# Gated cross-attention block: the order of the last two head pairs' scores, values and outputs

## The chip, the cores and the metric

The kernel runs on one NeuronCore of one Trainium2 chip. The metric is the device time of one execution in microseconds (us). Names of engines: TensorE (PE in the profile), VectorE (DVE), ScalarE (ACT), GpSimd (POOL), SyncE (SP), which here only issues DMAs.

## The reference

`x` (32 batches of 64 tokens, width 512) attends to a context of the same shape, and a feed-forward layer with LoRA adapters follows, both added back through a gate:

```python
x = x + tanh(g_xattn) * xattn(layernorm(x), ctx_4096, mask, bias)   # 32 heads of 128
x = x + tanh(g_ffn) * ffn(layernorm(x))
# xattn: q = h @ Wq, k = c @ Wk, v = c @ Wv
#        p = softmax(q @ k.T / sqrt(128) + bias, masked);  return (p @ v) @ Wo
# ffn:   y = x @ weight.T + bias, plus (x @ A.T) @ B.T of the batch's adapter
```

All of it is float32. The kernel reaches that precision by splitting each operand into a high part and a low remainder and adding three products (high by high, high by low, low by high).

## The kernel before, in words

The 2048 tokens are done in two halves (`p` = 0 and 1) of 1024 tokens, which are 8 tiles of 128. A half has a stage A and an attention stage; after the second half the feed-forward layer runs in four chunks of 512 tokens.

**Stage A** computes the keys and the values of all 32 heads for this half and stores them in DRAM. Heads go in pairs (`n` = 0 to 15). The key product of one pair (`unit`, L354) is a Strassen-like scheme with seven products p1 to p7 instead of eight; each product needs one split block of the context (tiles `c1p` for the second half) and one split block of the weight (tiles `wk`). Their results appear as psum tiles px, py, pv, pz. The context blocks of the second half are made by `next_blocks` (L455) while the first half's attention is still ending: a split is a cast on ACT (L89) and a subtraction (L90) on GpSimd, or on VectorE where the code says so; plain subtractions of raw blocks are L468. It waits twice on `gate`: block p5 needs the first entry, blocks p2 and p4 the second, since they take over tiles that the attention's last outputs still read. The weight blocks come from `prep` (L305) and `key_blocks` (L566), sums L288, casts L295 and low parts L299, all of their sums and low parts on GpSimd.

**Attention** (`attention`, L745) handles head pairs in order. For a pair `n`:

- `q_unit(n)` makes the queries (psum px, py, pv, pz, tile `qT`).
- `score` (L1051) makes the scores `ps` on TensorE. VectorE adds the bias tile `sm` (L814) and takes the row maximum (L816), GpSimd subtracts it (L817), ACT takes the exponential (L826). The bias is loaded by `load_bias` (L756, 2 x 256 KB) into one of two `sm` buffers, which the pair two before must have left, and GpSimd adds the mask to it (`bias_mask`, L765).
- `normed` (L830) sums the rows on VectorE (L836 to L838) and scales them on GpSimd (L839).
- `turned` (L853) transposes the probabilities in blocks of 32 on VectorE (L850, tile `tp`), loads the bias of pair `n + 2`, and puts the blocks in place with 16 ACT copies of 32 x 256 (L847, tile `pt`; `pz` for pair 14). Its argument `pace` says how many copies go at each step. For the pairs 14 and 15 together `last_turned` (L898) does both, with the second head of pair 15 placed by VectorE directly (also L847).
- `pv(n, cs)` (L944) multiplies by the values into `po` (L949), in four groups of eight 128-wide matmuls, `c` being the half of the tokens. ACT evicts the high part (L953) and VectorE the low part (L954), into `ch` and `cl`, or, for pairs 13 and 15, both into `cx`.
- `oproj` and, for the last four pairs two by two, `oproj2` (L997) multiply by the output weights into `pa`, 6 matmuls per pair and tile, and VectorE adds them to the accumulator `acc` (L993, L1008). `oproj2(n, ts, lead)` first issues pair `n`'s matmuls for `lead` tiles, then those of pair `n + 1`. The weights are split by `prep_o` (L965, tile `wo`, ACT L89 and GpSimd L90); when a pair's weights are split, it fetches the next pair's on SP.

**What sets the order.** [...] TensorE's order is written out by hand in `run` (L1022). The work of the other engines hangs on generators in the list `streams`; `beat()` (L64), called after each group of matmuls, advances each of them by one step. `paced(g, k)` takes a step only at every k-th beat. `drain(g)` issues all that is left of a generator at once. So the position of a stream's start decides where its instructions stand in the queues of ACT, VectorE, GpSimd and SP.

In the kernel before, the end of a half's attention is, in this order: outputs of pair 11, queries 14, values 12, queries 15, then `last_unit()` (it starts the blocks and first keys of the next half, or in the second half the splitting of the feed-forward weights, `ffn_weights`, L1158), scores of 14 and 15, values 13, outputs of 12 and 13 for six tiles, values of 14 and 15 for the first half of the tokens, outputs of 12 and 13 for the other two tiles, values of 14 and 15 for the second half, outputs of 14 and 15. In the second half `beside` (L1295) puts two things between the tiles of those last outputs: VectorE's normalization (`ffn_norm`, L132) and moments (L105, L106) and, by `ffn_tile` (L1185), TensorE's transposes of the first chunk (`tpf`, evicted to `fa`). The adapter product `ffn_lora` (psum `pt`, L1197) follows and needs all four of these.

Of the kernel before, what the change touches and what calls it, by code (L numbers as in the profile page):

```python
# [23 lines left out]
NPH = 2  # L24
# [19 lines left out]
def flamingo_block(ctx: ExitStack, tc: tile.TileContext, x, xT, ctxT, bias, mask, gx, gf,  # L44
# [410 lines left out]
    def next_blocks(f, tags, nm, out, gate):  # L455
# [22 lines left out]
        while not gate:  # L478
            yield
        yield from block("p5", b11)  # L480
        while len(gate) < 2:
            yield
        yield from block("p2", b21, nc.vector)
        yield from sub(b21, b21, b22, nc.vector)
        yield from block("p4", b21, nc.vector)

# [258 lines left out]
    def attention(p, res, rest, qt, freed):  # L745
# [152 lines left out]
        def last_turned():  # L898
# [14 lines left out]
            for k in range(16):  # L913
                if k in (1, 3, 6, 8):
                    next(norm)
                if k in (4, 5):
                    turn_next(n, k - 4)
                if k in (5, 7):
                    zero(k // 7)
                if k == 9:  # L920
                    turn_next(n + 1, 0)
                if k > 5:
                    for of, m, i, q in todo[:3]:
                        copy(nc.scalar.copy, m, i, of, *q)
                    del todo[:3]
                if k > 10:
                    for m, i, q in direct[:2]:
                        copy(nc.vector.transpose, m, i, sm[m % 2][:, i], *q)
                    del direct[:2]
                yield  # L930
# [6 lines left out]
        def ctx_of(n):  # L937
# [4 lines left out]
            return ch, cl  # L942

        def pv(n, cs=(0, 1)):  # L944
            drain(b["s", n])
            for i, c in [(i, c) for i in range(2) for c in cs] if n == 0 else [(i, c) for c in cs for i in range(2)]:
                ps = psum(f"po{p}_{n}_{i}_{c}")
# [8 lines left out]
            if n + 1 < NPR - 1:  # L956
                load_v(n + 1)
                if ("n", n + 1) in b:
                    drain(b["n", n + 1])
                    b["s", n + 1] = turned(n + 1)  # L960
                    next(b["s", n + 1])
                    next(b["s", n + 1])
                    streams.append(b["s", n + 1])

        def prep_o(n):  # L965
# [5 lines left out]
            b["o", n] = t  # L971
            for i in range(2):
                sl = slice(i * 512, (i + 1) * 512)
                split(raw[:, sl], t[:, 0, sl], t[:, 1, sl], nc.gpsimd)
                yield
# [46 lines left out]
        def run(xq, prefetch, before_last, last_unit, values_read, beside=None):  # L1022
# [8 lines left out]
            def q_unit(n):  # L1031
# [13 lines left out]
                end()  # L1045
                if n == NPR - 1:
                    last_unit()
                elif n % 2 and n > 3:
                    start_q(n + 1)
# [38 lines left out]
            for a in range(4, NPR, 2):  # L1088
# [8 lines left out]
                if a < NPR - 2:  # L1097
                    pv(a - 1)
                score(a, a + 1)
                if a == NPR - 8:  # L1100
                    streams.append(paced(prefetch(), 4))

            n = NPR - 4
            load_v(n + 3)
            pv(n + 1)
            start_o(n + 2)
            oproj2(n, range(6), 3)
            start_o(n + 3)
            for c in range(2):
                if c:  # L1110
                    oproj2(n, range(6, NT), 1)
                pv(n + 2, (c,))
# [129 lines left out]
    for p in range(NPH):  # L1242
# [10 lines left out]
        if p < NPH - 1:  # L1253
# [10 lines left out]
            def last_unit():  # L1264
                nonlocal blocks
                blocks = paced(next_blocks(f, qt, f"c{p + 1}", first[0], gate), 2)
                keys = prep("k", g, nc.gpsimd, 34, then=lambda: fetch("k", g + 2, "r0"))
                streams.extend((blocks, keys))
# [8 lines left out]
        else:  # L1277
# [17 lines left out]
            def beside(t):  # L1295
                if t < 4:
                    ffn_norm(0, t)
                    moments(t)
                else:
                    ffn_tile(0, t - 4)  # L1300
                if t == 4:
                    rstd_of(NPH * NCH - 2)

            def rest_of(t):
                if t < 2:
                    moments(4 + 2 * t)
# [57 lines left out]
```

## Time and profile before

| | |
|---|---|
| median of 3 runs | 1549.71 us (1549.27 to 1550.78) |
| the profiled execution | 1549.48 us, span of its instructions 1547.70 us |
| TensorE busy | 1529.2 us (99%), mean granted clock 0.996 |
| VectorE, ScalarE, GpSimd busy | 948.0 (61%), 719.2 (46%), 1041.8 (67%) |
| first half: values 13 begin / next half's first key product | 677.68 / 742.58 |
| second half: values 13 begin / first transpose of chunk 1 | 1412.78 / 1480.73 |

Times are counted from the first instruction of the span. The busy share of TensorE comes from pipelined matmuls, so it does not say that TensorE works at its peak; where it truly waits is in the timeline, in brackets ahead of the instruction that waited. The granted clock is 1.00 at full speed and 0.50 when the array's clock is halved.

### The profile page before, as it was taken

How to read it: one execution, taken by the hardware profiler on the slowest of the kernel's cores; microseconds unless marked ns; L12 is line 12 of the kernel's file. 1: busy time of each engine (PE TensorE's matmuls, PEld its weight loads, DVE VectorE, ACT ScalarE, POOL GpSimd, SP SyncE). 2: the span in 40 equal slices, each digit the busy share in tenths (PEclk: the TensorE clock that was granted, in tenths of full speed). 3: DMA queues.
4: the chain of work that ended last, by engine and by line, in shares of the span. 5: the costliest groups of instructions: out<-in, count | busy, mean ns of one | idle time of the engine just before them, and what ended most of it. 6: DMA issues, size and time to landing. Idle time of an engine off the chain costs nothing.

```text
span 1547.7 us, 25053 instructions
## 1 busy us (share of the span) xinstructions
PE 1529.2 (99%) x8988; PEld 1285.1 (83%) x8988; DVE 948.0 (61%) x1583; ACT 719.2 (46%) x1586; POOL 1041.8 (67%) x1152
## 2 busy tenths in 40 slices
PE   9999999999999999999999999999999999999899
PEld 7888888888888888877788888888888888888777
DVE  5665554376576657655486558437657665766654
ACT  6444233355664565464334423335566456547321
POOL 3898478968666666666689847896866666666210
PEclk9999999999999999999999999999999999999999
DMA  5754544484243444441475454438425344444111
GB/s 212 264 191 150 199 169 171 142 315 163 89 173 136 145 169 163 152 137 55 146 276 191 150 200 170 171 142 310 162 90 181 132 149 165 167 147 131 42 41 69
DMA packets 111071, 248.51 MB, mean 161 GB/s; under 512 B 10241, under 2 KB 44033, under 8 KB 106850
## 3 DMA queue, kind: packets, MB, share of 16 engines
q1 hardware_dynamic: 110658, 246.38, 45.7%
q8 instruction: 71, 1.16, 0.3%
q10 hardware_dynamic: 288, 0.52, 0.1%
q14 instruction: 54, 0.44, 0.1%
HBM read 173.45 MB, written 73.42 MB: 160 GB/s over the span
## 4 chain that ended last, share of the span: by engine, by line
PE 91%; DVE 3%; POOL 2%; issue 1%; DMA 1%; ACT 1%; SPq 0%; DVEq 0%; POOLq 0%; ACTq 0%
PE pa L98 21%; PE po L949 7%; PE pzv L98 6%; PE pvv L98 6%; PE pxv L98 6%; PE pzk L98 5%; PE pvk L98 5%; PE pxq L98 5%; PE pxk L98 5%; PE pzq L98 5%; PE pvq L98 5%; PE ps L812 3%; PE pyv L98 3%; PE pyq L98 3%; PE pyk L98 3%; PE pf L98 2%
## 5 line engine op out<-in xcount | busy, mean ns | idle before, releaser
L98 PE MATMUL pa<-wo,ch 128*128 128x512 f32 x896 | 280.3, 394 | 0.0
L847 ACT COPY pt<-tp 32x256 f32<-32x256 f32 x456 | 183.9, 403 | 64.0 <-DVE tp L850 53.0
L98 PEld LDWEIGHTS pa<-wo,ch 128*128 128x128 f32 x896 | 167.5, 189 | 34.8
L98 PE MATMUL pa<-wo,cl 128*128 128x512 f32 x448 | 175.5, 392 | 0.0
L993 DVE TENSOR_TENSOR acc<-pa,acc 128x512 f32<-128x512 f32 x192 | 129.3, 681 | 53.5 <-PE pa L98 53.5
L765 POOL TENSOR_TENSOR sm<-sm,madd 128x512 f32<-128x512 f32 x60 | 76.7, 1294 | 103.9 <-DMA sm<-bias 103.9
L949 PE MATMUL po<-pt,v 128*128 128x128 f32 x960 | 115.4, 278 | 8.5 <-ACT pt L847 4.4
L949 PEld LDWEIGHTS po<-pt,v 128*128 128x128 f32 x960 | 113.5, 194 | 11.8 <-ACT pt L847 5.7
L839 POOL TENSOR_TENSOR sm<-sm,r 128x512 f32<-128x512 f32 x64 | 66.9, 1045 | 77.5 <-DVE r L838 70.0
L954 DVE TENSOR_TENSOR cl<-po,ch 128x512 fp32r<-128x512 f32 x112 | 76.4, 691 | 47.4 <-ACT ch L953 47.0
L356 DVE TENSOR_TENSOR vt<-pvv,vt 128x512 f32<-128x512 f32 x64 | 44.1, 689 | 93.3 <-PE pvv L98 93.2
L98 PEld LDWEIGHTS pa<-wo,cl 128*128 128x128 f32 x448 | 84.5, 189 | 18.5 <-DVE cl L954 0.6
L90 POOL TENSOR_TENSOR wo<-rawo,wo 128x512 fp32r<-128x512 f32 x64 | 81.4, 1295 | 21.6 <-ACT wo L89 21.6
L817 POOL TENSOR_TENSOR sm<-sm,mx 128x512 f32<-128x512 f32 x64 | 67.0, 1050 | 40.8 <-DVE mx L816 40.8
L953 ACT CAST ch<-po 128x512 fp32r<-128x512 f32 x112 | 65.6, 590 | 59.7 <-PE po L949 58.0
L356 DVE TENSOR_TENSOR qT<-pvq,qT 128x512 f32<-128x512 f32 x64 | 44.1, 690 | 73.2 <-PE pvq L98 73.1
L356 DVE TENSOR_TENSOR kT<-pvk,kT 128x512 f32<-128x512 f32 x60 | 41.3, 688 | 71.6 <-PE pvk L98 71.4
L378 ACT COPY vt<-pxv 128x512 f32<-128x512 f32 x32 | 18.9, 589 | 131.0 <-PE pxv L98 131.0
L826 ACT ACTIVATE sm<-sm 128x512 f32<-128x512 f32 x60 | 38.0, 633 | 83.9 <-POOL sm L817 80.7
L356 DVE TENSOR_TENSOR qT<-pzq,qT 128x512 f32<-128x512 f32 x64 | 44.2, 691 | 37.8 <-PE pzq L98 37.6
L812 PEld LDWEIGHTS ps<-kB,qT 128*64 128x64 f32 x2048 | 61.3, 138 | 4.2 <-issue 2.1
L812 PE MATMUL ps<-kB,qT 128*64 128x64 f32 x2048 | 64.1, 223 | 0.3 <-DVE qT L356 0.3
(997 smaller groups left out, 3879.5 us busy)
## 6 DMA issues: line engine op xcount, KB each, us to landing
kd<-kT SPq DMA_DIRECT2D x64, 512.0 KB, 3.6
vd<-vt SPq DMA_DIRECT2D x128, 256.0 KB, 2.3
kB<-kd SPq DMA_DIRECT2D x32, 1024.0 KB, 9.7
v<-vd SPq DMA_DIRECT2D x32, 1024.0 KB, 7.7
rawq<-wq SPq DMA_DIRECT2D x32, 512.0 KB, 3.4
sm<-bias SPq DMA_DIRECT2D x64, 256.0 KB, 6.3
rawo<-wo SPq DMA_DIRECT2D x32, 512.0 KB, 3.6
rawk<-wk SPq DMA_DIRECT2D x31, 512.0 KB, 5.4
```

Source lines behind the costliest of these rows:

```text
L90: eng.tensor_tensor(lo, raw, hi.bitcast(F32), ALU.subtract)
L98: nc.tensor.matmul(ps, a, b, start=start and i == 0, stop=stop and i == 3 * n - 1, skip_group_check=True)
L356: nc.vector.tensor_tensor(o, ps, i, ALU.add)
L765: nc.gpsimd.tensor_tensor(t, t, masks[p][0], ALU.add)
L812: nc.tensor.matmul(ps[h * S:(h + 1) * S, t, :], qT[:, i, tok], kT[:, i, tok], start=True, stop=True)
L817: nc.gpsimd.tensor_tensor(s, s, mx.unsqueeze(2).to_broadcast([P, NT, S]), ALU.subtract)
L839: nc.gpsimd.tensor_tensor(t, t, r.unsqueeze(2).to_broadcast([P, NT, S]), ALU.mult)
L847: f(pts[n == NPR - 2][dst, i, :, src], of[src, :, ki * 32:(ki + 1) * 32])
L949: nc.tensor.matmul(ps[:, t * P:(t + 1) * P], b["v", n][:, c * 4 + t, i * P:(i + 1) * P], pts[n == NPR - 2][:, i, c * 4 + t, :], start=True ...
L953: nc.scalar.copy(h[:, i, sl], ps)
L954: nc.vector.tensor_tensor(lo[:, i, sl], ps, h[:, i, sl].bitcast(F32), ALU.subtract)
L993: nc.vector.tensor_tensor(acc[t], ps, acc[t], ALU.add)
```

## The change

Six edits, all at the two ends of attention:

1. In `pv` of pair 12, pair 13 is turned (its VectorE transposes and the load of pair 15's bias) before the values of pair 12 instead of behind them; the copies keep their place behind the values.
2. Ahead of the scores of 14 and 15, the rest of pair 13's copies and the two casts of its output weights are issued, and then all streams are set aside; they come back after the values of 13. `last_unit()` moves there too, from the end of queries 15.
3. All eight tiles of outputs 12 and 13 come before the values of 14 and 15, the first four tiles as one group.
4. `last_turned` normalizes at steps 0, 2, 6 and 8 rather than 1, 3, 6 and 8.
5. In `next_blocks`, the subtraction for block p4 goes to GpSimd before the second gate, and the split of p4 goes from VectorE to GpSimd. The wait of the first keys' stream goes from 34 to 18 beats.
6. In the second half, the transposes of the first feed-forward chunk come at the tiles 2 to 5 of the last outputs rather than 4 to 7, and the moments of the tiles 0 to 3 after tile 3; the scales of chunk 2 (15 small GpSimd steps) move into the first chunk.

```diff
@@ -478,11 +478,11 @@
         while not gate:
             yield
         yield from block("p5", b11)
+        yield from sub(b22, b21, b22)
         while len(gate) < 2:
             yield
         yield from block("p2", b21, nc.vector)
-        yield from sub(b21, b21, b22, nc.vector)
-        yield from block("p4", b21, nc.vector)
+        yield from block("p4", b22)
 
     f = [big(f"f{j}", [P, KT, 512], F32, f"c0_{j}") for j in range(2)]
     fetch("k", 0, "r0", 4)
@@ -911,7 +911,7 @@
                 nc.vector.memset(pts[1][h * S:(h + 1) * S, :, :, (1 - h) * S:(2 - h) * S], 0.0)
 
             for k in range(16):
-                if k in (1, 3, 6, 8):
+                if k in (0, 2, 6, 8):
                     next(norm)
                 if k in (4, 5):
                     turn_next(n, k - 4)
@@ -941,8 +941,17 @@
                 return more_ctx
             return ch, cl
 
+        def turn_pair(n, **pace):
+            drain(b["n", n])
+            b["s", n] = turned(n, **pace)
+            next(b["s", n])
+            next(b["s", n])
+
         def pv(n, cs=(0, 1)):
             drain(b["s", n])
+            if n == NPR - 4:
+                turn_pair(n + 1, pace=(0, 1, 2, 2, 3, 2, 2, 2, 2))
+                next(b["s", n + 1])
             for i, c in [(i, c) for i in range(2) for c in cs] if n == 0 else [(i, c) for c in cs for i in range(2)]:
                 ps = psum(f"po{p}_{n}_{i}_{c}")
                 for t in range(4):
@@ -956,10 +965,8 @@
             if n + 1 < NPR - 1:
                 load_v(n + 1)
                 if ("n", n + 1) in b:
-                    drain(b["n", n + 1])
-                    b["s", n + 1] = turned(n + 1)
-                    next(b["s", n + 1])
-                    next(b["s", n + 1])
+                    if n != NPR - 4:
+                        turn_pair(n + 1)
                     streams.append(b["s", n + 1])
 
         def prep_o(n):
@@ -969,9 +976,16 @@
             else:
                 t = kqp.tile([P, 2, 1024], F32R, tag="kq", name=f"wo{p}_{n}")
             b["o", n] = t
-            for i in range(2):
-                sl = slice(i * 512, (i + 1) * 512)
-                split(raw[:, sl], t[:, 0, sl], t[:, 1, sl], nc.gpsimd)
+            halves = [slice(i * 512, (i + 1) * 512) for i in range(2)]
+            if n == NPR - 3:
+                for sl in halves:
+                    nc.scalar.copy(t[:, 0, sl], raw[:, sl])
+                yield
+            for sl in halves:
+                if n == NPR - 3:
+                    nc.gpsimd.tensor_tensor(t[:, 1, sl], raw[:, sl], t[:, 0, sl].bitcast(F32), ALU.subtract)
+                else:
+                    split(raw[:, sl], t[:, 0, sl], t[:, 1, sl], nc.gpsimd)
                 yield
             if n + 1 < NPR:
                 fetch("o", p * NPR + n + 1, "r1")
@@ -1043,9 +1057,7 @@
                 if n == 1:
                     start_o(0)
                 end()
-                if n == NPR - 1:
-                    last_unit()
-                elif n % 2 and n > 3:
+                if n % 2 and 3 < n < NPR - 1:
                     start_q(n + 1)
 
             def score(*ns):
@@ -1096,19 +1108,28 @@
                 start_o(a - 1)
                 if a < NPR - 2:
                     pv(a - 1)
+                else:
+                    drain(b["s", a - 1])
+                    next(ob[a - 1])
+                    held = list(streams)
+                    streams.clear()
                 score(a, a + 1)
                 if a == NPR - 8:
                     streams.append(paced(prefetch(), 4))
 
             n = NPR - 4
             load_v(n + 3)
+            beat()
+            streams.append(ob[n + 1])
+            drain(ob[n + 1])
             pv(n + 1)
+            streams.extend(g for g in held if g is not ob[n + 1])
+            last_unit()
+            oproj2(n, range(4), 4)
             start_o(n + 2)
-            oproj2(n, range(6), 3)
+            oproj2(n, range(4, NT), 1)
             start_o(n + 3)
             for c in range(2):
-                if c:
-                    oproj2(n, range(6, NT), 1)
                 pv(n + 2, (c,))
                 pv(n + 3, (c,))
             values_read(acc)
@@ -1264,7 +1285,7 @@
             def last_unit():
                 nonlocal blocks
                 blocks = paced(next_blocks(f, qt, f"c{p + 1}", first[0], gate), 2)
-                keys = prep("k", g, nc.gpsimd, 34, then=lambda: fetch("k", g + 2, "r0"))
+                keys = prep("k", g, nc.gpsimd, 18, then=lambda: fetch("k", g + 2, "r0"))
                 streams.extend((blocks, keys))
 
             def values_read(acc):
@@ -1295,13 +1316,14 @@
             def beside(t):
                 if t < 4:
                     ffn_norm(0, t)
-                    moments(t)
                 else:
-                    ffn_tile(0, t - 4)
-                if t == 4:
+                    moments(t - 4)
+                if 1 < t < 6:
+                    ffn_tile(0, t - 2)
+
+            def rest_of(t):
+                if t == 0:
                     rstd_of(NPH * NCH - 2)
-
-            def rest_of(t):
                 if t < 2:
                     moments(4 + 2 * t)
                     moments(5 + 2 * t)
```

## The prediction

> **What bounds the kernel now.** I read the page first, then TensorE's own waits, the busy time by stretch, and the timelines of TensorE and GpSimd around the end of each attention half.
>
> ```profile
> PE 1529.2 (99%) x8988; PEld 1285.1 (83%) x8988; DVE 948.0 (61%) x1583; ACT 719.2 (46%) x1586; POOL 1041.8 (67%) x1152
> ...
> 588.03:660.60 72.57, 72.57 (x463) 61.74 (x463) 49.44 (x89) 41.43 (x94) 48.05 (x54) 1.00 0.44 153
> 677.68:742.58 64.90, 58.84 (x293) 49.25 (x289) 34.14 (x59) 28.00 (x60) 42.50 (x41) 0.95 0.28 93
> 1412.78:1480.73 67.95, 62.85 (x317) 51.93 (x313) 40.77 (x75) 26.82 (x55) 26.69 (x37) 0.95 0.19 62
> ```
>
> TensorE sets the time. In a regular stretch (588 to 661) it is busy without a gap at full clock, so only removed waits can gain. The two ends of attention, from pair 13's values on, hold idle time and a mean clock of 0.95. TensorE's timeline (start, duration, line, operation, in brackets the idle time before it):
>
> ```profile
> 686.88 1.22 PE L98 MATMUL pa<-wo,cx 128*128 128x512 f32 x3 [1.26 <-ACT cx L953]
> 689.10 5.12 PE L98 MATMUL pa<-wo,cx 128*128 128x512 f32 x15 [1.00 <-ACT cx L953]
> ...
> 706.31 1.16 PE L949 MATMUL po<-pt,v 128*128 128x128 f32 x8 [2.14 <-ACT pt L847]
> 709.13 1.98 PE L949 MATMUL po<-pt,v 128*128 128x128 f32 x8 [1.66 <-DVE pt L847]
> ...
> 1438.23 1.16 PE L949 MATMUL po<-pt,v 128*128 128x128 f32 x8 [2.25 <-ACT pt L847]
> 1441.25 2.08 PE L949 MATMUL po<-pt,v 128*128 128x128 f32 x8 [1.85 <-DVE pt L847]
> ```
>
> TensorE waits for pair 13's evicted context and then for the turned probabilities of pair 15. After each wait matmuls run at half speed (15 in about 5 us; normally 12 take 2.72). GpSimd shows why the softmax is late:
>
> ```profile
> 676.44 2.52 POOL L765 TENSOR_TENSOR sm<-sm,madd 128x512 f32<-128x512 f32 x2 [10.08 <-DMA sm<-bias]
> 678.90 1.05 POOL L817 TENSOR_TENSOR sm<-sm,mx 128x512 f32<-128x512 f32 x1
> 679.90 1.29 POOL L90 TENSOR_TENSOR c1p<-c,c1p 128x512 fp32r<-128x512 f32 x1
> 681.13 1.31 POOL L90 TENSOR_TENSOR wo<-rawo,wo 128x512 fp32r<-128x512 f32 x1
> 682.38 1.06 POOL L817 TENSOR_TENSOR sm<-sm,mx 128x512 f32<-128x512 f32 x1
> ...
> 1375.66 1.05 POOL L817 TENSOR_TENSOR sm<-sm,mx 128x512 f32<-128x512 f32 x1 [0.27 <-DVE mx L816]
> ```
>
> Pair 15's bias lands so late that its mask additions stand in front of the first max subtraction (L817), and splits (L90) stand between the others. In an ordinary pair (last line) they follow VectorE at 1.32 us each.
>
> **The Trainium skill.** "TensorE: Matmul & The Clock Gate", Part 1: the array's clock is halved after an idle window of about 3.4 us and comes back after a busy one, and the window runs freely. Here the half-clock stretches are 3.4 us (at 688.8 and 709.3) and 6.8 us (at 1439.7); the windows ahead of the first two were about a third and under a third busy, so a window need not be wholly idle. The same page, Architectural detail: ScalarE, VectorE and GpSimd take their work strictly in order, which agrees with L817 behind L90 above. "SBUF — State Buffer", two separate sides: VectorE with two SBUF inputs and GpSimd lock each other out; here 256-wide GpSimd steps take 0.74 us, and 1.17 to 1.23 beside VectorE's subtractions at 749 to 753.
>
> **The change, part by part.** Prices: output matmul 2.72/12 = 0.227 us; a pair's values 3.57 for both halves, 1.78 for one; GpSimd 1.29 (L90, L765, L468), 1.05 (L817, L839); ACT 0.48 to 0.53 per queued 512-wide cast, 0.415 per turned copy; VectorE 0.6 to 0.7 per 512-wide step.
>
> *1. Pair 13 turned ahead of pair 12's values.* The two VectorE transposes (1.30) move from 665.65 to about 661.4, behind the last addition of q14. The four evictions of pair 12 slip by at most 0.4 us; their outputs are not read before 681. SP: the two bias loads go out at about 662.8 rather than 668.08, now ahead of wo13 (512 KB), v13 and k16, which can't start before 666.4 anyway. At 6.3 to 8.3 us they land by 671, so the two mask additions are over by 673 and free GpSimd before the first maximum at 676.47. The copies still start after pair 12's values are read, and end at 675.2 as now, because eight of them stand behind the px copy that TensorE releases at 671.2.
>
> *2. No other stream among the scores.* GpSimd's four L817 then follow VectorE's maxima: 676.5, 677.8, 679.2, 680.5, ending at 681.55 (now 687.9). wo13's casts (2 x 0.6) run ahead of the exponentials, its two subtractions behind the first L839: 681.6 + 1.05 + 2.58 = 685.2. Pair 13's four casts queue behind the last exponential (682.1) and end at 684.2, their low halves at about 686.4.
>
> *3. Order on TensorE.* From 677.68: values 13 (3.57) to 681.3; pair 12's terms of tiles 0 to 3, 24 x 0.227 = 5.44, to 686.7. Then pair 13's terms: the first half's low parts are there at 684.1, wo13 at 685.2. No wait, with 1.5 us to spare. All eight tiles end at 703.0. Meanwhile the last two pairs turn: VectorE does the row sums (1.1 each), four turns or clears and the additions in order, the last direct transposes end at about 699; ACT makes 24 copies (9.96) and a few casts from 687.1, ending at about 699. TensorE asks for pair 14 at 703.0 (ready 694.8) and for pair 15 at 704.8 (ready 699). Both waits go, by about 6 us. The earlier last_turned steps (0 and 2 for 1 and 3) are in these times.
>
> *4. Output weights.* On SP wo14's load goes out behind wo13's subtractions (685.2; now 684.7), v14's behind it, landing near 693.3 at its 7.7 us, used at 703. wo14 is split behind the 24 copies, ready at 701.9; wo15's load follows it and lands 3.6 us later at 705.6, its low half is ready at 708.8 behind two more block subtractions. It is asked for at 710.2 + 2.72 = 712.9. ACT waits for that load between two casts of pair 14, which have 4 us to spare.
>
> *Sum.* From values 13: 3.57 + 96 x 0.227 + 4 x 1.78 + 96 x 0.227 = 54.2. The first half now takes 742.58 - 677.68 = 64.9: gain **10.7**. In the second half, 1412.78 to 1480.73 = 67.95 now; after, 54.2 + four transposes inside the tiles at 0.49 (3.21 less 2.72 in the trace) + the adapter's 8 x 0.227 = 58.0: gain 9.95. Its bias load and L817s move as in the first half, and its weight splits come after the copies.
>
> *5. Second half's tail.* The tiles of chunk 0 are turned two steps earlier, so the adapter's waits at 1478 (0.68, 0.22) go (already in the 9.95). New: the moments of tile 3 (0.8) stand between the last addition and the normalization that the next transpose needs: last matmul + 0.2 + 0.6 + 0.8 + 0.54 = 2.2 against 1.8 of adapter matmuls: 0.4 lost, leaving 9.55. GpSimd's 15 small steps for the scales (4.2 us) move later; their first reader is some 7 us behind.
>
> *6. Blocks of the next half.* The block stream starts nine beats later, and the key stream's own wait falls from 34 to 18. GpSimd has about 41 us of work from 681.6 to the first key product at 731.9, some 9 us of slack; k16 is ready near 720, and k17's load (SP, behind wo15's split at 708.8) has 20 us. Block p4's subtraction (2 x 1.29) goes there unhurried. But p4's own split moves from VectorE to GpSimd, in a place where TensorE already waits: now p4's product ends at 753.92 instead of 752.1. After: cast at 750.7, subtraction to 752.05, then a key sum (0.74) releases a key cast that stands in ACT ahead of p4's second cast (753.7), subtraction to 755.0, product at 755.5. Loss **1.6**. GpSimd is 2.6 us later for the key blocks behind, which lead by 4.4. Within these 4.1 us TensorE is busy 0.7, so about half the phases of a 3.4 us window halve the clock next, at 1.7: book 0.9. Bounds: -1.8 (nothing left to wait for) and +4.
>
> Total: 10.7 + 9.55 - 1.6 - 0.9 = 17.7. The profiled execution took 1549.48 us (span 1547.70 and 1.78 around it), 0.23 under the median. 1549.5 - 17.7 = **1531.8**.
>
> **Rivals.**
> - *The turning is still late* (15%). If only the bias delay went, the chain from the end of the scores to the last direct transpose would stay near 31.3 and 28.4 us (709.1 - 677.75; 1441.2 - 1412.8), against 27.1 that TensorE needs to pair 15: 4.2 + 1.3 of wait and one or two slow windows: 7 to 9 us back, 1540. For it: VectorE has new additions in the way. Against it: the L817s alone gain 6.3.
> - *The wait moves to wo15* (12%). Its load now leads its use by 11 us, before by 25. If GpSimd runs 6 us late, TensorE waits 2 to 3 us per half, perhaps with a slow window: 1537.
> - *Slower: GpSimd bounds the next key stage* (6%). A key unit costs it 11 x 0.74 = 8.1 of 9.52 us. The p4 splits put it behind; if it then met VectorE's lock often enough that a step's mean passed (9.52 + 1.3)/11 = 0.98 us for 15 units, the gain would be gone. At 1.18 us (13.0 per unit) in half of the units: 7 x 3.5 = 24.5, 1556. Against it: those VectorE subtractions leave the stage here.
> - *The order changes and nothing else* (1%), 1549.5: excluded if the waits are gone at all.
>
> The forecast itself has 66%, its own range 1529 to 1535. The floor, with every wait and slow window removed, is 1549.5 - 10.7 - 9.95 - 1.8 = 1527. The range 1528 to 1539 leaves out the slower case and half of the late turning. Faster by over 0.2% (about 3 us, what a measurement of this kernel can tell from no change): 0.93; within it 0.01; slower 0.06.
>
> **What would show it.** Right: L817 in steps of 1.3 us behind the maxima, the bias landing before 672, no wait before po of pair 15, clock 1.00 in both ends, 54 us from values 13 to the next key product, p4's product waiting for GpSimd at the start of the key stage. Wrong: bracketed waits at po or cx, half-clock windows there, GpSimd-released waits at pxk or pyk, or a wait for rawo.

## The result, and the profile after

| us | before | after |
|---|---|---|
| median (range), 5 runs each on one chip | 1549.27 (1547.70 to 1550.78) | **1532.18** (1530.62 to 1533.45) |
| profiled execution, its span | 1549.48, 1547.70 | 1530.62, 1528.82 |
| first half: values 13 to the next half's first key product | 64.90 | 54.39 |
| from there to the second half's values 13 | 670.21 | 671.99 |
| second half: values 13 to the first transpose of chunk 1 | 67.95 | 58.61 |
| rest of the span behind it | 66.97 | 66.63 |

The ratio of after to before is 0.989, with a 95% interval of 0.9876 to 0.9904: 17.1 us by the medians, where 17.7 were predicted. The two profiled spans differ by 18.88: gains of 10.51 and 9.34 in the two attention ends, 0.34 behind them and 0.47 ahead of them (where nothing was changed), less a loss of 1.78 in the key stage.

TensorE and GpSimd in the first line of the page (busy time, share of the span, instructions):

```profile
PE 1519.3 (99%) x8988; PEld 1280.5 (84%) x8988; DVE 941.6 (62%) x1579; ACT 718.4 (47%) x1586; POOL 1046.7 (68%) x1156
```

Busy time by stretch in the kernel after (start and end, length, then PE, PEld, DVE, ACT and POOL busy, granted clock, DMA share, GB/s):

```profile
677.21:731.59 54.38, 54.38 (x291) 46.86 (x289) 33.92 (x59) 28.20 (x61) 43.13 (x40) 1.00 0.33 111
731.59:745.00 13.41, 10.79 (x45) 7.98 (x44) 4.51 (x7) 6.39 (x15) 8.38 (x10) 1.00 0.05 20
1403.58:1462.18 58.60, 58.29 (x316) 49.77 (x313) 40.25 (x76) 26.48 (x55) 21.99 (x20) 1.00 0.22 72
```

The first and third lines are the two ends of attention. TensorE is now busy without a gap in the first and, but for 0.31 us, in the second, both at full clock. The gaps that are left have moved to the middle line, the start of the next key stage: 10.79 busy of 13.41. TensorE's timeline of the kernel after, where the waits were before and where the new ones are (brackets hold the idle time ahead of the instruction and what ended it):

```profile
686.35 5.60 PE L98 MATMUL pa<-wo,cx 128*128 128x512 f32 x24
...
702.67 1.95 PE L958 MATMUL po<-pz,v 128*128 128x128 f32 x16
704.46 1.95 PE L958 MATMUL po<-pt,v 128*128 128x128 f32 x16
...
741.11 0.73 PE L98 MATMUL pvk<-c1p,wk16p 128*128 128x512 f32 x2 [0.85 <-POOL c1p L90]
742.75 0.50 PE L98 MATMUL pvk<-c1p,wk16p 128*128 128x512 f32 x1 [0.92 <-ACT c1p L89]
744.11 0.74 PE L98 MATMUL pvk<-c1p,wk16p 128*128 128x512 f32 x2 [0.85 <-POOL c1p L90]
...
1434.40 1.95 PE L958 MATMUL po<-pt,v 128*128 128x128 f32 x16
...
1462.18 0.63 PE L137 MATMUL tpf<-ident,xn 128*128 128x128 f32 x4 [0.31 <-DVE xn L132]
```

Pair 13's terms (`cx`) run as one group of 24 without a bracket, 5.60 us instead of 18 matmuls with two waits. The values of pair 15 (`po<-pt`) wait in neither half: 16 matmuls in 1.95, where two times eight stood with waits of about 2 us ahead of each. New are three waits of 0.85 to 0.92 for block p4 (`pvk<-c1p`) and 0.31 for the normalization of the last tile.

GpSimd's timeline of the kernel after:

```profile
665.83 2.55 POOL L765 TENSOR_TENSOR sm<-sm,madd 128x512 f32<-128x512 f32 x2
676.07 1.04 POOL L817 TENSOR_TENSOR sm<-sm,mx 128x512 f32<-128x512 f32 x1 [7.68 <-DVE mx L816]
677.38 1.04 POOL L817 TENSOR_TENSOR sm<-sm,mx 128x512 f32<-128x512 f32 x1 [0.27 <-DVE mx L816]
678.71 1.04 POOL L817 TENSOR_TENSOR sm<-sm,mx 128x512 f32<-128x512 f32 x1 [0.28 <-DVE mx L816]
680.02 1.04 POOL L817 TENSOR_TENSOR sm<-sm,mx 128x512 f32<-128x512 f32 x1 [0.28 <-DVE mx L816]
```

The mask additions (L765) are over almost eight microseconds before the first maximum needs GpSimd, and the four L817 follow VectorE in steps of 1.3 us. The direct transposes that end the softmax of pair 15, from VectorE's timeline of the kernel after:

```profile
698.11 0.90 DVE L847 STREAM_TRANSPOSE pt<-sm 32x256 f32<-32x256 f32 x2
```

In the kernel before, the same pair stands here:

```profile
708.18 0.89 DVE L847 STREAM_TRANSPOSE pt<-sm 32x256 f32<-32x256 f32 x2
```

They end at 709.07 there, and TensorE waits for them until 709.13. In the kernel after they end at 699.01, and TensorE starts the group that reads them at about 704.46 + 0.89 = 705.4. So 6 us are to spare.

### The profile page after: what moved, and what is told of

It reads as the page before. It is cut to its first block, busy times and chain, and to the rows that moved or that the text cites. A ratio compares the mean times of both kernels' runs of the same rounds, so it can differ in the third digit from the quotient of the medians.

```text
span 1528.8 us, 25060 instructions
## 1 busy us (share of the span) xinstructions
PE 1519.3 (99%) x8988; PEld 1280.5 (84%) x8988; DVE 941.6 (62%) x1579; ACT 718.4 (47%) x1586; POOL 1046.7 (68%) x1156
## 3 DMA queue, kind: packets, MB, share of 16 engines
q8 instruction: 71, 1.16, 0.3%
## 4 chain that ended last, share of the span: by engine, by line
PE 96%; DVE 1%; POOL 1%; ACT 1%; issue 1%; DMA 0%; DVEq 0%; ACTq 0%; POOLq 0%
PE pa L98 23%; PE po L958 7%; PE pzv L98 6%; PE pvv L98 6%; PE pxv L98 6%; PE pxq L98 5%; PE pzq L98 5%; PE pvq L98 5%; PE pzk L98 5%; PE pvk L98 5%; PE pxk L98 5%; PE ps L812 4%; PE pyv L98 3%; PE pyq L98 3%; PE pyk L98 3%; PE pf L98 3%
## 5 line engine op out<-in xcount | busy, mean ns | idle before, releaser
L765 POOL TENSOR_TENSOR sm<-sm,madd 128x512 f32<-128x512 f32 x60 | 76.7, 1291 | 89.4 <-DMA sm<-bias 89.4
L817 POOL TENSOR_TENSOR sm<-sm,mx 128x512 f32<-128x512 f32 x64 | 67.0, 1048 | 57.2 <-DVE mx L816 57.0
L90 POOL TENSOR_TENSOR wo<-rawo,wo 128x512 fp32r<-128x512 f32 x60 | 76.0, 1289 | 16.7 <-ACT wo L89 16.7
L378 ACT COPY vt<-pxv 128x512 f32<-128x512 f32 x32 | 18.8, 588 | 131.0 <-PE pxv L98 131.0
L192 POOL TENSOR_TENSOR vs<-wvr,wvr 128x512 f32<-128x512 f32 x24 | 31.7, 1333 | 48.0 <-DMA wvr<-wv 48.0
```

The lines of the kernel that those rows point to most:

```text
L90: eng.tensor_tensor(lo, raw, hi.bitcast(F32), ALU.subtract)
L765: nc.gpsimd.tensor_tensor(t, t, masks[p][0], ALU.add)
L817: nc.gpsimd.tensor_tensor(s, s, mx.unsqueeze(2).to_broadcast([P, NT, S]), ALU.subtract)
```

## The experiments

The theory: what counts is when the chain from the scores to the turned probabilities of pair 15 ends, against the moment at which TensorE asks for them. The chain has two ends: the last of ACT's copies, which the first eight matmuls of `po<-pt` read, and the last direct transpose on VectorE, which the next eight read. The change moves both sides: the work put in front of the values moves the asking later, the quiet streams and the early turn move the chain's end earlier. Its price is p4's split on GpSimd. The main rivals are that one edit alone does it, or that the new waits are not p4's doing. In each result the four stretches of the table above stand in the same order, from the profiled execution.

### One part alone, from the kernel before

*The order of the outputs alone*, with three tiles in the first group:

```diff
-            oproj2(n, range(6), 3)
+            oproj2(n, range(NT), 3)
             start_o(n + 3)
             for c in range(2):
-                if c:
-                    oproj2(n, range(6, NT), 1)
```

> The kernel before with one edit: all eight tiles of outputs 12+13 come before the values of 14 and 15 (two tiles later than now, group of three kept); nothing else of the change. My account, in which order and the earlier softmax both count: the first wait, at cx behind 18 matmuls, stays (4.6 us in the first half with its slow window, 1 in the second), the wait at the values of pair 15 all but goes, since TensorE asks 5.4 us later for a chain that ends 31.3 and 28.4 us behind the scores: 1535 to 1538. Rival, the order is nothing without the early softmax: 1545 or more, waits of several us at po of pair 15. Rival, the order is everything: 1533 or less.

1536.32 us (1535.43 to 1536.69), ratio 0.9919 (0.9902 to 0.9935); stretches 58.53, 670.27, 60.84, 66.97. As expected: a few lines of order alone bring 12.9 us of the 17 (1549.24 for the kernel before beside it). By the brackets of TensorE's timeline, 1.31 + 1.00 us of wait stay ahead of pair 13's terms and 0.40 ahead of the values of pair 15.

*The same with a first group of four tiles* (`oproj2(n, range(NT), 4)`):

> The kernel before with the new order and a first group of four tiles instead of three (24 matmuls of pair 12 ahead of pair 13's, as in the change); softmax and streams as before. My account: what the order alone left (58.5 us in the first half) is the lateness of the softmax, whose exponentials hold up pair 13's evictions to about 690: six more matmuls shorten the wait at cx by 1.4 us, and TensorE then waits that much longer for pair 15: first half 57.5 to 58.6, second 60 to 61, whole 1535 to 1537, no real difference to the group of three. Rival, the lead of 24 matmuls is what the order lacked: 54.4 to 56 in the first half, 1533 or less.

1535.26 us (1534.67 to 1535.91), ratio 0.991 (0.9894 to 0.9927); stretches 58.39, 670.24, 61.17, 66.95. TensorE's timeline of this kernel:

```profile
688.75 5.33 PE L98 MATMUL pa<-wo,cx 128*128 128x512 f32 x21 [1.02 <-ACT cx L953]
...
709.42 1.16 PE L949 MATMUL po<-pt,v 128*128 128x128 f32 x8 [1.79 <-DVE pt L847]
```

The fourth tile takes 1.29 us from the waits ahead of `cx`, and the wait ahead of the values grows by 1.39. The first half gains only 0.14. A wait is not saved where it shrinks, only where the last one of its chain shrinks.

*The early turn alone:*

```diff
...
         def pv(n, cs=(0, 1)):
             drain(b["s", n])
+            if n == NPR - 4:
+                turn_pair(n + 1, pace=(0, 1, 2, 2, 3, 2, 2, 2, 2))
+                next(b["s", n + 1])
...
```

> The kernel before with one edit: pair 13 is turned, and pair 15's bias loaded, ahead of the values of 12; the order, the streams and the rest as before. My account: the masks are out of the way by 669, so the last max subtraction ends near 684.3 as in the run with streams on, 3.6 us earlier than in the kernel before. TensorE then still asks too early by 2 us or more at cx (behind 18 matmuls) and by about 2 at po of pair 15: first half 58 to 60.5 us from values 13 to the next key product (64.9 before, 54.4 in the change), second 61 to 64 (67.95), whole 1537 to 1541. Rival, the late bias is the whole cause: 55.5 or less in the first half, 1534 or less. Rival, it is nothing without order or streams: 63 or more, 1546 or more.

A **miss**: 1543.89 us (1543.03 to 1544.49, six runs), ratio 0.9965 (0.9954 to 0.9977); stretches 63.25, 670.23, 64.75, 66.96. TensorE's timeline of this kernel shows the same law:

```profile
686.60 4.01 PE L98 MATMUL pa<-wo,cx 128*128 128x512 f32 x15 [0.44 <-ACT cx L962]
...
703.80 1.19 PE L958 MATMUL po<-pt,v 128*128 128x128 f32 x8 [3.25 <-ACT pt L847]
706.61 2.08 PE L958 MATMUL po<-pt,v 128*128 128x128 f32 x8 [1.62 <-DVE pt L847]
```

The waits ahead of `cx` shrank from 2.26 to 0.44, where the expectation had 2 or more left, but TensorE then came earlier to the values, and those waits grew from 3.80 to 4.87. The expectation was wrong in two places. It had the last max subtraction end 3.6 us earlier; counted from the values of 13 it ended 2.4 earlier (7.9 us behind them for 10.2), because four splits still stood between the subtractions (three in the run with the streams left running, below, from which the 3.6 was taken), and the chain's end, the last direct transpose, came earlier by the same 2.4 (29.0 for 31.4). And it left out the half clock behind the last wait, which lasted 5.0 us here and 3.4 before. So the stretch gained 1.65.

### One part undone, in the kernel after

*Two tiles of outputs back between the values* (`oproj2(n, range(4, 6), 1)`, then `range(6, NT)` with `start_o(n + 3)` ahead of the second half of the tokens):

> The changed kernel with the last two tiles of outputs 12+13 put back between the two halves of the values of 14 and 15, everything else kept (wo15's split starts behind the first half's values). My account: TensorE then asks for pair 15 at about 698.6 on the changed kernel's clock, where the last ACT copy and direct transpose end at 698.6 and 699.0: a wait of up to 1 us per half, no slow window, 1532 to 1534. Rival, the order is what hides the chain: 3 to 5 us of wait per half with slow windows, 1540 or more.

1532.30 us (1531.12 to 1533.70), ratio 0.9894 (0.9879 to 0.9909); stretches 54.40, 673.30, 58.62, 66.63. No wait returns in the two ends, where up to 1 us was expected. The extra 1.3 us in the key stage are a half clock (743.9 to 747.3) behind p4's waits.

*Pair 13 turned behind the values of 12 again* (the three lines of `pv` taken out, `turn_pair(n + 1)` without its condition):

> The changed kernel with pair 13 turned behind the values of pair 12 again. My account: the load of pair 15's bias goes out at about 667.5 and its masks are added at 676 to 678.5, so the four max subtractions end about 2 us later than in the change (683 for 681), and wo13's low parts at about 686.8 for 684.8, which is 0.2 us behind TensorE's asking (686.6): up to 0.5 us of wait at pa in the first half, none at pair 15 (asked at 704.5, ready by 701.5): 1532 to 1533.5. Rival, the late bias is the cause of the whole lateness: waits at po come back, 1538 or more.

1533.49 us (1532.67 to 1534.01), ratio 0.9901 (0.9886 to 0.9916); stretches 54.39, 674.81, 58.61, 66.64. The mask additions wait 10.63 us for the bias again and the four L817 run from 679.02 to 683.08 rather than from 676.07 to 681.06, yet the first half is as short as in the kernel after. The extra 2.8 us in the key stage are a half clock behind p4's waits, shown below.

*The streams left running among the scores*, `last_unit()` back at the end of queries 15, with the blocks one beat later and the keys' wait at 27; the copies of pair 13 and the casts of its output weights still go out ahead of the scores:

```diff
...
                     next(ob[a - 1])
-                    held = list(streams)
-                    streams.clear()
...
-            streams.append(ob[n + 1])
             drain(ob[n + 1])
             pv(n + 1)
-            streams.extend(g for g in held if g is not ob[n + 1])
-            last_unit()
...
```

> The changed kernel with the other streams running among the scores again: they are not set aside, and last_unit() is back at the end of queries 15 (the block stream one beat later and the keys' wait 27, so that blocks and keys meet the next key stage in the same places). Turning early and the new order are kept. My account: splits stand between the max subtractions again, which end 2 to 4 us later than in the change, but with the bias landed early; the turned probabilities are ready at 701 to 703 for TensorE's 704.5: first half 54.4 to 56 us from values 13 to the next key product (54.39 in the change), whole 1532 to 1534. Rival, setting the streams aside is what removes the waits: first half 58 us or more, whole 1537 or more.

1532.22 us (1531.07 to 1532.58), ratio 0.9881 (0.9866 to 0.9895); stretches 54.39, 671.93, 58.61, 66.62. GpSimd's timeline of this kernel (its L821 is L817 before, L990 a weight's low half):

```profile
678.85 1.04 POOL L821 TENSOR_TENSOR sm<-sm,mx 128x512 f32<-128x512 f32 x1
679.85 1.28 POOL L90 TENSOR_TENSOR c1p<-c,c1p 128x512 fp32r<-128x512 f32 x1
681.10 1.27 POOL L990 TENSOR_TENSOR wo<-rawo,wo 128x512 fp32r<-128x512 f32 x1
682.33 2.04 POOL L821 TENSOR_TENSOR sm<-sm,mx 128x512 f32<-128x512 f32 x2
```

The splits stand between the subtractions again, which end at 684.37 instead of 681.06. The chain ends 25.5 us after the values of 13 begin, still before TensorE asks.

*Both the late turn and the two tiles between the values* (streams still set aside):

> The changed kernel with two parts undone together: pair 13 is turned behind the values of 12, and the last two tiles of outputs 12+13 are back between the values. Each alone cost no wait at all at the values. My account: they are each other's reserve. The direct transposes ended at 700.8 with the late turn; with the two tiles moved back TensorE asks for them at about 699.9, so waits of 1 to 2 us per half return at po of pair 15, without a half-clock window: first half 55 to 56.5, whole 1533.5 to 1537. Rival, setting the streams aside is enough alone: no wait, 54.4, 1532 to 1533.5.

1534.10 us (1532.44 to 1535.14), ratio 0.9893 (0.9878 to 0.9908); stretches 55.67, 674.49, 59.30, 66.60. Now a wait is back, in TensorE's timeline of this kernel:

```profile
700.25 2.05 PE L955 MATMUL po<-pt,v 128*128 128x128 f32 x16 [0.98 <-ACT pt L847]
```

Here TensorE waits for ACT's copies, not for the direct transposes. The extra 2.5 us in the key stage are again a half clock (744.1 to 750.9).

The table puts the first halves together. All times count from the start of the values of 13. "Asked" is when TensorE would read if nothing waited: 27.25 for the copies and 28.14 for the direct transposes, as in the kernel after, or 21.81 and 22.70 with two tiles fewer in front, as the run with two tiles back shows without a wait. "Late by" is the larger of the two.

| kernel | last copy: ready, asked | last direct transpose: ready, asked | late by | first half |
|---|---|---|---|---|
| before | 28.6, 21.8 | 31.4, 22.7 | 8.7 | 64.90 |
| early turn alone | 26.2, 21.8 | 29.0, 22.7 | 6.3 | 63.25 |
| order alone, group of three | 28.7, 27.3 | 32.1, 28.1 | 4.0 | 58.53 |
| order alone, group of four | 28.5, 27.3 | 32.0, 28.1 | 3.8 | 58.39 |
| after, late turn and two tiles back | 22.9, 21.8 | 23.3, 22.7 | 1.1 | 55.67 |
| after, two tiles back | 21.5, 21.8 | 21.8, 22.7 | in time | 54.40 |
| after, late turn | 23.2, 27.3 | 23.5, 28.1 | in time | 54.39 |
| after, streams running | 22.5, 27.3 | 25.5, 28.1 | in time | 54.39 |
| after | 21.4, 27.3 | 21.8, 28.1 | in time | 54.39 |

The first half is 54.4 plus what the chain is late by, within 0.2, except for 1.8 and 2.5 more in the first two lines. That is the half clock behind the last wait: 3.4 and 5.0 us at half speed, which cost 1.7 and 2.5. The same sum holds in the second half: in the kernel before, 58.6 + 5.7 late + 2.6 of half clock + 1.0 for the tail (below) make 67.9, and 67.95 was measured.

No part is the cause by itself, because the parts overlap. Of the 10.5 us in the first half, the order alone took 6.5 and the early turn alone 1.65. The quiet scores with the earlier normalization steps, without the early turn and with the two tiles back, took 9.2; that kernel keeps the group of four, which in the two runs of the order alone was worth 0.14. With the others in place, setting the streams aside, the early turn, or the last two tiles ahead of the values can each be undone at no cost in these stretches.

The earlier normalization steps were never undone alone, but the traces show that something behind the subtractions counts too. From the end of the last max subtraction to the last direct transpose it takes 21.2 us before and with the early turn alone, 21.8 with the order alone in a group of four, 18.0 in the kernel after, and 18.8 there with the streams running. So more than 2 of the 9.6 us by which the chain ends earlier don't come from the streams, the order or the early turn. What is left are parts of the change that no run undoes alone, such as the normalization steps or the casts of pair 13's output weights sent ahead; which of them it is stays open.

### The tail of the second half

*The transposes and moments of the first chunk at their old places*, all else as after; one run:

> The changed kernel with the last part undone: the transposes of the first feed-forward chunk at tiles 4 to 7 of the last outputs again, the moments at tiles 0 to 3. My account: the waits of 0.68 and 0.22 us ahead of the adapter product return with its two slow starts, the 0.31 us at tpf goes: second half 59.2 to 59.6 us from values 13 to the first transpose of chunk 1, for 58.61. Rival: with the rest of the change the last outputs no longer leave these waits, 58.3 to 58.6.

1534.05 us; stretches 54.39, 673.57, 59.57, 66.96. TensorE's timeline of this kernel:

```profile
1462.84 0.50 PE L1218 MATMUL pt<-fa,a 128*128 128x512 f32 x1 [0.67 <-ACT fa L1210]
1463.56 0.50 PE L1219 MATMUL pt<-fa,a 128*128 128x512 f32 x1 [0.22 <-DVE fa L1211]
```

The adapter's two waits are back. The edit is worth 59.57 - 58.61 = 0.96 and another 0.3 behind it. The key stage of this one execution holds a half clock (745.8 to 749.3), so its total is not to be set beside the median of the kernel after.

### The price: block p4

*p4's split on VectorE again*, its subtraction left on GpSimd:

```diff
-        yield from block("p4", b22)
+        yield from block("p4", b22, nc.vector)
```

> The changed kernel with one part undone: block p4's split is back on VectorE, while its subtraction stays early on GpSimd. My account: TensorE's 3.5 us at p4's product (3 waits at pvk) come from two GpSimd subtractions of 1.27 us in series with a GpSimd key sum and an ACT key cast between them. On VectorE (0.69 each) and with that sum no longer behind them, the waits shrink to 0.8 us or less: 2.7 us faster than the change, about 1529.3, and the half-clock window that four of its five runs seem to hold (mean clock 0.998 against 0.999 in the fifth) should be gone from nearly all runs, for another 1 to 1.5 us. Rival: the waits belong to the tiles that p4 takes over from the last outputs, not to the engine that splits; then the place stays at 3 us or more and the time at 1532. A second rival: TensorE waits next for key blocks that VectorE or ACT now delays, and under 1 us is gained.

1528.94 us (1528.73 to 1530.17), ratio 0.9874 (0.9859 to 0.9889); stretches 54.39, 669.97, 58.61, 66.62. TensorE's timeline of this kernel:

```profile
742.57 0.97 PE L98 MATMUL pvk<-c1p,wk16p 128*128 128x512 f32 x3 [0.73 <-DVE c1p L90]
743.72 0.72 PE L98 MATMUL pvk<-c1p,wk16p 128*128 128x512 f32 x2 [0.18 <-DVE c1p L90]
```

2.62 us of waits became 0.91, and the key stage is 2.0 us shorter. The four runs all have a mean clock of 1.000, four of the five runs of after 0.998.

*p4 without any wait*: also a block at every beat, not every second, once the second gate is open:

```diff
...
-    def paced(g, k):
+    def paced(g, k, hurry=lambda: False):
         for _ in g:
             yield
             for _ in range(k - 1):
-                yield
+                if not hurry():
+                    yield
...
-                blocks = paced(next_blocks(f, qt, f"c{p + 1}", first[0], gate), 2)
+                blocks = paced(next_blocks(f, qt, f"c{p + 1}", first[0], gate), 2, lambda: len(gate) > 1)
...
```

First together with the moments of tile 3 moved behind the normalization that TensorE waits for at 1462:

> The changed kernel improved: p4's split on VectorE, and the block stream takes a step on every beat once the last gate is open, so that p4's casts stand ahead of ACT's copy of px instead of behind it; and the moments of tile 3 move behind the normalization that the first transpose of chunk 1 waits for. My account: the 0.9 us of wait left at p4 with VectorE alone go, and with them 1.5 us (from values 13's key product to the second half's values 13: 668.4 to 669.0 us, against 669.97 and 671.99), and the 0.31 us wait at tpf goes (second half 58.3 for 58.61): 1526.8 to 1527.6, clock 1.0 in all runs. Rival: the casts now stand in front of ACT's key casts and the next key product waits for those: 1529 or more.

1527.65 us (1527.47 to 1527.71), ratio 0.9852 (0.9836 to 0.9869); stretches 54.39, 668.37, 58.14, 67.42. The key stage has no wait left at p4. The moved moments missed: they gave 0.47 in the second half and took 0.79 in the rest, where they stand ahead of the next chunk's normalizations. So the next run left them where the change puts them, beside the unedited kernel after on the same chip:

> As e7, but the moments of tile 3 stay where the change has them. My account: in e7 moving them gained 0.47 us before the first transpose of chunk 1 and lost 0.79 behind it, because three moments then stood ahead of the next eviction and normalization on VectorE; so this is 0.3 us faster than e7: rest after that transpose 66.6 us for e7's 67.42, second half 58.6 for 58.14, whole 1527.0 to 1527.6. Rival: the tail is free, no difference or slower than 1527.7.

> The changed kernel itself, unedited, beside e11 on the same chip. My account: 1531 to 1533.5, its runs spread by whether the wait at p4 brings a half-clock window (mean clock 0.998 and 0.999 against 1.0 in e11's runs), 4 to 6 us slower than e11, of which 3.6 us is p4's waiting and 1 to 2 the window. Rival: p4's gain was one chip's, under 3 us between the two.

**1527.34 us** (1527.16 to 1527.47), ratio to before 0.9864 (0.9847 to 0.988), stretches 54.39, 668.36, 58.60, 66.59; the kernel after beside it 1532.86 (1531.03 to 1533.38), 0.9897 (0.9883 to 0.9912), stretches 54.39, 671.93, 58.61, 66.59. This is the fastest of all the kernels run, and close to the 1527 that the prediction named as the floor. TensorE's timeline of the version with p4 early:

```profile
740.08 1.52 PE L98 MATMUL pvk<-c1p,wk16p 128*128 128x512 f32 x6
741.43 1.52 PE L98 MATMUL pzk<-c1p,wk16p 128*128 128x512 f32 x6
```

p4's product is one group of six in 1.52 us. Of the 5.5 us between the two medians, 3.6 are in the key stage of the profiled executions; those two also differ by 1.5 ahead of the values of 13, where their code is alike, which is spread. Whether a half clock in the untraced runs makes up the rest stays open.

## Why the prediction was right

The predicted 1531.8 stands 0.4 us from the median, and the forecast case came in for the reasons given.

1. *Early turn.* Right, and better than booked: VectorE turned at 660.93, the loads went out at 661.66 and 662 and landed 3.8 us later (the prediction took 6.3 to 8.3), so the additions ran at 665.83, ten microseconds before the old 676.44.
2. *Quiet scores.* The four L817 were forecast to start at 676.5 and end at 681.55; they did at 676.07 and 681.06. wo13's low halves were ready at 684.8 (685.2), pair 13's four casts at 683.7 (684.2).
3. *Order.* Pair 13's terms were asked for at 686.35 (686.7 forecast), pair 14 at 702.67 (703.0), and the chain ended at 699.01 (699). The first stretch was 54.39 against 54.2 worked out, the second 58.61 against 58.4.
4. *Output weights.* ACT waited 0.89 us for wo15's load, as said; the cast came at 705.24 (705.6), wo15 was ready at 708.5 (708.8) and asked for at 712.55 (712.9).
5. *Tail.* 0.31 lost of the 0.4.
6. *Key stage.* p4's product ended 13.10 us after the first key product began (744.69 - 731.59); the prediction has 755.5 - 742.58 = 12.92, and 11.34 before. The waits are where it put them. The loss was 1.78 against 1.6.

The term that was undersized is the **half clock behind p4**: booked at 0.9, as one time in two at 1.7. Seven profiled executions have p4's split on GpSimd as in the kernel after, and four of them show it, for 1.3 (two tiles back), 1.6 (tail back), 2.5 (late turn and two tiles back) and 2.8 us (late turn). The profiled execution of after had none, but four of its five runs have a mean clock of 0.998 and are 1.5 to 2.8 us longer than it, which would fit such a stretch; they have no trace, so that is inferred. The last section estimates from a trace that it comes in about three of four executions rather than one in two, which at the mean of these four costs is 1.6. Without that booking the predicted sum is 18.6; the two profiled executions, neither with a half clock in the key stage, differ by 18.86, of which 0.8 lies where the prediction expected no difference. So the parts came in for the reasons given, but that the total is off by only 0.4 is in part luck: this unforeseen 0.8 stands against the half clock that was booked too low.

Two readings of the lines in the prediction were loose, and neither carries the forecast. Matmuls don't run at half speed after each wait: in the two ends only three stretches have the half clock (688.8 to 692.2, 709.3 to 712.7, 1439.7 to 1446.5), and the eight matmuls at 1438.23 took 1.16 us at full speed. And in the 3.4 us ahead of the first two TensorE was busy 43% and 38%, rather than about a third and under a third.

The rivals: the late turning fell (the chain ended at 21.8 us after the scores, not at 28 to 31); with the late turn kept in the run above it would still have been in time. The wait for wo15 fell: ready 4 us before it was asked for. GpSimd did not bound the key stage: all of its loss lies ahead of 744.69. That the order changes nothing fell with the first stretch.

What the prediction did not see is the **reserve**. It gave the quiet scores and the early turn as conditions of the gain. The runs show that with the order changed either could have been left out, that the order without both still gives 12.9 to 13.8 of the 17 us, and that the change without the early turn and with two tiles back still gives 15.6 (1534.10 for 1549.66).

## What to carry to other kernels

Of several waits along one chain, compare only the chain's end with the moment at which the last reader asks: a wait removed further up comes back at the next one, and work put in front of the reader is worth as much as a shorter chain. Once the chain is in time, further edits to it earn nothing, so look next at what the change put into other stages: here p4's split cost 2.0 us more on GpSimd than on VectorE, since TensorE waits for it there, and on VectorE, issued earlier, it cost no wait at all.

## What the runs showed of the hardware that was not expected

The clock is halved after gaps that are each under a microsecond. TensorE's timeline of the kernel after with the late turn:

```profile
741.18 0.73 PE L98 MATMUL pvk<-c1p,wk16p 128*128 128x512 f32 x2 [0.85 <-POOL c1p L90]
742.83 0.50 PE L98 MATMUL pvk<-c1p,wk16p 128*128 128x512 f32 x1 [0.92 <-ACT c1p L89]
744.19 1.22 PE L98 MATMUL pvk<-c1p,wk16p 128*128 128x512 f32 x2 [0.85 <-POOL c1p L90]
745.21 2.76 PE L98 MATMUL pzk<-c1p,wk16p 128*128 128x512 f32 x6
747.77 2.73 PE L98 MATMUL pyk<-c1p,wk17p 128*128 128x512 f32 x6
750.33 1.55 PE L98 MATMUL pvk<-c1p,wk17p 128*128 128x512 f32 x6
```

Groups of six take 2.7 us instead of 1.5 until about 750.3: a stretch of 6.8 us that begins at 743.5, inside the last of three gaps of at most 0.92. The Trainium skill ("TensorE: Matmul & The Clock Gate", Part 1) gives an idle window of about 3.4 us as what halves the clock; here no gap comes near that length, and the measurement decides.

The traces show more. In all of them the granted clock changes only on a grid of 3.413 us. Cut into the windows of this grid, the 14 traces (without their first 15 and last 5 us) hold nine windows at full clock in which TensorE was busy for less than half, 29 to 49.6%. All nine were followed by half clock. None of the twenty windows that were busy 51 to 75% was. Four windows at half clock that were busy 52 to 83% were followed by another at half clock; the nine that were busy 87% or more were followed by full clock. Three windows at p4's waits:

| kernel | window (us) | TensorE busy | clock in the next window |
|---|---|---|---|
| after, late turn | 740.10 to 743.51 | 1.47 (43%) | 0.50 |
| after, late turn and two tiles back | 740.67 to 744.08 | 1.69 (49.6%) | 0.50 |
| after | 742.04 to 745.45 | 1.84 (54%) | 1.00 |

So in these traces the busy share of a window tells whether the next is halved, and what counts is where the windows fall on the gaps: much the same gaps left the clock at 1.00 in the kernel after, which agrees with the page's free-running window. The limit is a regularity of these traces. No run was made to test it, and the ends of matmuls in a profile are modelled, so one half is good to a few hundredths.

An estimate follows from it. If windows of 3.413 us are laid on the trace of the kernel after at every possible offset, 77% of the offsets put a window that is busy for less than half on p4's waits. With p4's split on VectorE no offset does (the least is 73% busy), which fits the mean clock of 1.000 in its four runs.
